# A graph layer with a Fourier-domain convolution: left-over products prepared beside the layer norm, a fourth bank and token halves in the last gate, set-up on ScalarE, weights read in 2 KB runs

## The chip, the cores and the metric

The kernel runs on one core of one Trainium2 chip. The time is the device time of one execution in microseconds; lower is better. All data are float32.

## The reference

The input is 32 images of 512 tokens with 256 features, and one 512 x 512 adjacency per image. Cut to what matters:

```
h = maximum(layernorm(x), 0)
c = relu(bn1(conv1(h)))                 # 1 tap, 256 -> 256 channels
c = bn2(conv2(c))                       # 17 taps along the tokens, 256 -> 256
x_conv = relu(c + h)
s = h @ w_se.T + b_se                   # 3 features
A = exp(-dist(s)) * adj
msg = relu(h @ w_msg.T + b_msg)
x_nmp = A @ msg
gi = concat(x_conv, x_nmp) @ w_ih.T + b_ih ; gh = h @ w_hh.T + b_hh
r = sigmoid(gi_r + gh_r) ; z = sigmoid(gi_z + gh_z)
n = tanh(gi_n + r * gh_n)
out = x + (1 - z) * n + z * h
```

## The kernel before, in words

The convolution with 17 taps is done in the frequency domain. The tokens are cut into windows of 64, transformed with length 80 by a matrix product, multiplied by transformed weights, and transformed back. 40 "units" of two spectrum rows each (a real and an imaginary part) stand for the 80 rows. The 32 images form two groups (g = 0, 1) of 16.

The stages follow each other as follows.

1. `first_part(0)`, about 0 to 176 us: for each image the layer norm (`statistics` and `normalise`: DVE, with a `pow` on POOL), the transpose of h on TensorE (`transpose_h`, tile `phT`), relu into `hT`, `conv1` and `windows_to_freq`. Between them `weights_to_freq` transforms the 17-tap weights (products `pw` from the taps `w2p`) and stores them into the DRAM buffer `WD` (in the profile `wd`), one row per spectrum row.
2. `nodes(0)`, to about 467 us: per image `message`, `features`, `factors`, `affinity`, `aggregate` for x_nmp, and between these the complex products of the units, `product(g, u)`. A product needs its unit's weights from `wd` (`load_unit`, an SP DMA into one of three `wt` buffers), their sum `wsum` and two tiles `both` (three POOL operations, `prepare`). Three units (`LEFT = 3`: 37, 38, 39) are left over.
3. `first_part(1)`, to about 604 us: the layer norm stage of the second group. The three left-over products are spread in it by the helper `fill`, to give TensorE work while the layer norm begins. Units 37 and 38 are prepared ahead of the stage; unit 39 is prepared, weights' load included, only where its product stands.
4. `nodes(1)`, to about 904 us, with all 40 products of the second group.
5. The "late" part, to the end: 16 pairs of images. `inverse` transforms back, `gates_rz` forms r and z, `gate_n` forms n. The three matrix products of a gate over a pair of images (2 x 2 blocks) are done with seven block products instead of eight (`Q1` to `Q7`); the helper `into` issues the three matmuls of one block product into a PSUM bank. A result (i, j) is feature half i of image j of the pair.

`blend` (L695) then takes d = h - n, multiplies it by z and adds n. `finish` turns the result to token order (`to_tokens`, a DVE transposition), adds it to x and stores it; `between(i)` calls it for the pair before. In the last pair, z comes last: `early_out` adds n to x beforehand, and the nested function `then` adds the z part. It uses `gates_rz` with `outs=[1]`, which holds three banks: b1 (Q1, Q2), b2 (Q6, Q7, Q4), b3 (Q5, Q3).

The order: parts 1, 3 and 5 are issued as written (`manual_schedule`); elsewhere a scheduler orders the instructions. Each engine takes its instructions in order, as does each DMA queue (SP's, ScalarE's and POOL's). A DMA that waits holds up what is behind it on its queue. [...]

At set-up, bn1 is folded into conv1: `batch_norm` forms scale and shift per channel, four small products with `diag` matrices spread them over all partitions (`row1`), and `w1` is multiplied by the scale.

Lines that the text below speaks of: L110 loads of x; L160 to L182 the set-up; L237 `pw`; L250 stores into `wd`; L265 to L277 layer norm; L288, L289 transposes of h and relu (`hT`), L290 its store; L301 conv1; L328 loads of `wt`; L332 `wsum`; L345 and L346 `both`; L364 the units' products; L566 all gate products; L598 and L607 the sums u2 and u3 of two block products (both named u); L585 the last sum of a gate result, L581 its sigmoid; L674 h - n; L697 and L698 `blend`; L704 the transposition to tokens; L709 and L693 additions into x; L714 stores of the output; L765 the combination of the gate weights; L911 the multiplication by z in the last pair.

Of the kernel before, what the change touches and what calls it, by code (L numbers as in the profile page):

```python
# [57 lines left out]
def gnn_layer(  # L58
# [64 lines left out]
    load_rows(w1, w1T, nc.scalar)  # L123
# [24 lines left out]
    def vectors():  # L148

        for h in range(2):  # L150
            rows = slice(64 * h, 64 * (h + 1))
            nc.vector.tensor_copy(vech[rows].rearrange("p (m e) -> p e m", e=DC),
                                  vec2[rows].rearrange("p e (m h) -> p e m h", h=2)[..., h])
        for name in VEC:
            at[name] = vech[:, cols[name]]
        nc.vector.tensor_add(brz, at["b_ih"][:, : 2 * DC], at["b_hh"][:, : 2 * DC])
        batch_norm("bn2", scale2, shift2)

    def batch_norm(k, scale, shift):
        nc.vector.tensor_scalar(scale, at[k + "_v"], BN_EPS, None, op0=ALU.add)  # L160
        nc.gpsimd.tensor_tensor(scale, scale, minus_half[:, :DC], op=ALU.pow)
        nc.vector.tensor_mul(scale, scale, at[k + "_g"])
        nc.vector.tensor_mul(shift, at[k + "_m"], scale)
        nc.vector.tensor_sub(shift, at[k + "_b"], shift)

    scale1, shift1 = (consts.tile([P, DC], FP, name=f"bn1_{k}") for k in ("scale", "shift"))
    batch_norm("bn1", scale1, shift1)


    row1 = bank("row1")  # L170
    with tc.tile_pool(name="setup", bufs=2) as setup:
        ones = setup.tile([P, P], FP, name="ones", bufs=1)
        nc.vector.memset(ones, 1.0)
        for i, v in enumerate((scale1, shift1)):
            for c in range(DC):
                diag = setup.tile([P, P], FP, tag="diag", name=f"diag_{i}_{c}")
                nc.vector.tensor_scalar(diag, ident, v[:, c : c + 1], None, op0=ALU.mult)
                nc.tensor.matmul(row1[:, i * D + c * P : i * D + (c + 1) * P], ones, diag, start=True, stop=True)
    shift1_row = early.tile([P, D], FP, name="shift1_row")
    nc.vector.tensor_copy(shift1_row, row1[:, D : 2 * D])  # L180
    for c in range(DC):
        nc.vector.tensor_mul(w1[:, c, :], w1[:, c, :], row1[:, :D])  # L182
# [25 lines left out]
    WD = dram.tile([WROWS, D, D], FP, name="wd")  # L208
# [18 lines left out]
    def weights_to_freq(gen, pc, i):  # L227
# [19 lines left out]
        if s + per == SI:  # L247
            for q in range(4):
                i0 = QI * q + PI * pc + i + per - SI
                nc.sync.dma_start(WD[:, i0 : i0 + SI, :], WST[q])  # L250
# [74 lines left out]
    def load_unit(g, u):  # L325
        t = WT[g, u] = wts.tile([P, 2, DC, D], FP, tag="wt", name=f"wt_{g}_{u}")
        for k in range(2):
            nc.sync.dma_start(t[:, k], WD[2 * u + k].rearrange("(i p) o -> p i o", p=P))  # L328
# [234 lines left out]
    def into(bk, q, o, ks, terms, first):  # L563

        for i, k in enumerate(ks):
            nc.tensor.matmul(bk, sw[:, k, q, o, :], terms[k][q], start=(first and i == 0), stop=(i == len(ks) - 1),  # L566
# [5 lines left out]
    def gates_rz(p, terms, between, outs=range(2), then=lambda i, j: None):  # L572
# [10 lines left out]
        def result(bk, other, o, i, j):  # L583
# [3 lines left out]
            then(i, j)  # L587
# [11 lines left out]
        for o in outs:  # L599
            into(b1[o], Q2, o, ks, terms, False)  # L600
            sigmoid(b1[o], o, 0, 0)
            then(0, 0)
# [13 lines left out]
        for o in outs:  # L616
            into(b3[o], Q3, o, ks, terms, False)
            result(b3[o], u2[o], o, 0, 1)

    def gate_n(p, terms, last):  # L620
# [51 lines left out]
        for i, j in ((0, 0), (1, 1), (1, 0), (0, 1)):  # L672
# [4 lines left out]
            elif not last:  # L677
                blend(p, i, j)
# [11 lines left out]
    def late_out(p, i, j, engine):  # L690
        half = slice(32 * i, 32 * (i + 1))
        x = XP[p][j][:, :, half]
        engine.tensor_tensor(x, x, OUT[p, j][:, :, half], op=ALU.add)  # L693

    def blend(p, i, j):  # L695
        n, d = NT[p][:, i, j, :], RZ[p][:, i, j, :]
        nc.vector.tensor_mul(d, d, RZ[p][:, DC + i, j, :])  # L697
        nc.vector.tensor_add(n, n, d)  # L698
# [13 lines left out]
    def store(p, j, queues):  # L712
        for g in range(4):
            queues[g % len(queues)].dma_start(quarter(out[2 * p + j], g), XP[p][j][32 * g : 32 * (g + 1)])  # L714
# [6 lines left out]
    def first_part(g, freq, between, left=()):  # L721
# [7 lines left out]
        normalise(b0)  # L729
        left = list(left)  # L730

        def fill():
            if left:
                left.pop(0)()
# [4 lines left out]
        normalise(b0 + 1)  # L739
        for b in range(b0, b1):  # L740
            if b + 3 < b1:
                load_x(b + 3, nc.gpsimd)
            if b == b0:
                conv1(b)
                if g == 0:
                    for steps in between(0):
                        for step in steps:
                            step()
                fill()
# [33 lines left out]
    with tc.tile_pool(name="freq", bufs=1) as fpool:  # L783
# [63 lines left out]
        with phase("pw"):  # L847
            with phase("nodes"):
                nodes(0, xf, range(UNITS - LEFT), GB)
            with phase("first", "sums"):  # L850
# [10 lines left out]
                left = [partial(product, pools["pw"], 0, u, xf) for u in range(UNITS - LEFT, UNITS)]  # L861
                for u in range(UNITS - LEFT, UNITS - LEFT + 2):
                    prepare(pools["pw"], 0, u, xf)
# [7 lines left out]
    with phase("late"), phase("sw"), phase("ops", bufs=2), phase("work"), tc.manual_schedule():  # L871
# [9 lines left out]
        for p in range(pairs):  # L881
# [19 lines left out]
            else:  # L901


                def then(i, j):

                    d = RZ[p]
                    if (i, j) == (0, 1):
                        to_tokens(p, 0, 1, d[:, 1, 0, :])
                        late_out(p, 1, 0, nc.gpsimd)
                        store(p, 0, [nc.sync, nc.scalar])  # L910
                    nc.vector.tensor_mul(d[:, i, j, :], d[:, i, j, :], d[:, DC + i, j, :])  # L911
                    if (i, j) != (1, 0):
                        to_tokens(p, j, i, d[:, i, j, :])
                        late_out(p, i, j, nc.vector)
                    if (i, j) == (0, 1):
                        store(p, 1, [nc.sync, nc.scalar])

                gates_rz(p, terms, between, [0])
                gate_n(p, terms, True)

                def between(i):
                    early_out(p, 1 - i, 1)

                gates_rz(p, terms, between, [1], then)
# [38 lines left out]
```

## Time and profile before

| | |
|---|---|
| median of 3 runs | 1900.99 us (1900.66 to 1903.49) |
| the profiled execution, its own time | 1902.63 us |
| its span, first to last instruction | 1900.8 us |
| TensorE busy | 1849.6 us (97%) |
| VectorE (DVE) busy | 1085.9 us (57%) |
| ScalarE (ACT) busy | 597.9 us (31%) |
| GpSimd (POOL) busy | 578.3 us (30%) |
| DMA | 309.9 MB, mean 163 GB/s |
| mean granted TensorE clock | 0.990 |

The profile names instructions by line, engine, operation and tiles, written as output<-input. PE is TensorE, PEld its weight loads. In lists of waits the columns are: the engine and line that waited, what it waited for, us in total, number of times, longest. In a timeline they are: start in us, duration in us, engine, line, operation, tiles, shapes, count of merged instructions, and in brackets the idle time before and what ended it. In a table by stage they are: the stretch, its length, then for PE, PEld, DVE, ACT and POOL the busy time with the number of instructions, then the granted TensorE clock as a share of full speed, the busy share of the DMA engines, and GB/s. A list of one line's instructions gives minimum, median and maximum duration in ns.

### The profile page before, as it was taken

The page shows a single profiled execution, that of the slowest core. Times are in us where ns is not written, and L with a number is a line of the kernel's source. Part 1 is how long each engine was busy: PE and PEld are TensorE (multiplying, and loading weights), DVE is VectorE, ACT ScalarE, POOL GpSimd, SP SyncE. Part 2 cuts the span into 40 slices and gives each one's busy share as a digit, 9 for nine tenths or more (in the row PEclk, how much of TensorE's full clock was granted, in tenths as well). Part 3 has the DMA queues.
Part 4 walks back from the last instruction along what each step waited for, and adds up shares of the span by engine and source line. Part 5 has one row for each costly group of instructions (what it writes and reads, how often), then busy time and mean ns, then how long its engine had stood idle before and what let it go on. Part 6 is the DMA issues. An engine that isn't in the chain of part 4 may idle for free.

```text
span 1900.8 us, 20925 instructions
## 1 busy us (share of the span) xinstructions
PE 1849.6 (97%) x6976; PEld 1113.0 (59%) x6976; DVE 1085.9 (57%) x2170; ACT 597.9 (31%) x1147; POOL 578.3 (30%) x558
## 2 busy tenths in 40 slices
PE   7999999999799999999999999999999999999997
PEld 5767566665698667665545554555455554555443
DVE  6874645544685544544265456655665456655666
ACT  2456444433235434443212221222212221222121
POOL 3331333434332334444422322133212322133210
PEclk9999999999899999999999999999999999999999
DMA  7999998776467998888532554235522554245512
GB/s 204 295 266 232 250 264 239 225 218 205 150 238 194 251 268 260 235 227 245 164 83 52 126 131 117 53 92 130 130 77 54 130 130 104 59 98 130 130 27 40
DMA packets 336953, 309.89 MB, mean 163 GB/s; under 512 B 148567, under 2 KB 286711, under 8 KB 336463
## 3 DMA queue, kind: packets, MB, share of 16 engines
q1 hardware_dynamic: 310175, 232.09, 48.0%
q10 hardware_dynamic: 18992, 49.17, 7.3%
q0 software_dynamic: 7680, 27.30, 5.3%
q8 instruction: 56, 0.92, 0.2%
q14 instruction: 50, 0.41, 0.1%
HBM read 201.60 MB, written 106.89 MB: 162 GB/s over the span
## 4 chain that ended last, share of the span: by engine, by line
PE 82%; DVE 3%; DMA 1%; issue 1%; POOL 1%; ACT 0%; SPq 0%; DVEq 0%; POOLq 0%; ACTq 0%
PE pg L566 30%; PE pn L566 15%; PE pn L457 11%; PE py L364 10%; PE pc L555 6%; PE pm L408 5%; PE pc L301 2%; PE pd L443 2%; PE px L316 1%; DMA ws<-w 1%; PE psr L432 1%; PE phT L288 0%; DVE xn L277 0%; DVE stats L265 0%; DMA yd<-y 0%
## 5 line engine op out<-in xcount | busy, mean ns | idle before, releaser
L544 POOL TENSOR_TENSOR hp<-hp 128x512 f32<-128x512 f32 x64 | 95.4, 1501 | 463.0 <-DMA hp<-hd 419.7
L566 PE MATMUL pg<-hp,sw 128*128 128x512 f32 x448 | 229.8, 595 | 3.1 <-DVE u L598 3.1
L566 PE MATMUL pg<-np,sw 128*128 128x512 f32 x448 | 229.6, 594 | 0.0
L566 PE MATMUL pg<-cp,sw 128*128 128x512 f32 x448 | 228.8, 592 | 0.0
L457 PE MATMUL pn<-A,msg 128*128 128x512 f32 x512 | 225.0, 592 | 0.0
L457 PEld LDWEIGHTS pn<-A,msg 128*128 128x128 f32 x512 | 97.1, 190 | 110.6 <-issue 107.9
L364 PE MATMUL py<-wt,both 128*128 128x256 f32 x624 | 152.3, 387 | 9.0 <-POOL both L346 8.3
L581 ACT ACTIVATE rz<-rz,brz 128x512 f32<-128x512 f32 x96 | 69.3, 722 | 277.0 <-DVE rz L585 277.0
L345 POOL TENSOR_TENSOR both<-xf 128x256 f32<-128x256 f32 x78 | 60.8, 780 | 314.0 <-PE py L364 281.2
L566 PEld LDWEIGHTS pg<-hp,sw 128*128 128x128 f32 x448 | 85.0, 190 | 110.3 <-issue 100.2
L566 PEld LDWEIGHTS pg<-np,sw 128*128 128x128 f32 x448 | 85.4, 191 | 107.7 <-issue 107.7
L566 PEld LDWEIGHTS pg<-cp,sw 128*128 128x128 f32 x448 | 85.3, 190 | 107.7 <-issue 107.7
L364 PEld LDWEIGHTS py<-wt,both 128*128 128x128 f32 x624 | 115.2, 192 | 52.3 <-issue 27.3
L544 POOL TENSOR_TENSOR cp<-cp 128x512 f32<-128x512 f32 x64 | 80.5, 1268 | 183.7 <-ACT cp L560 182.5
L449 DVE TENSOR_TENSOR A<-e,at 128x512 f32<-128x512 f32 x128 | 109.2, 892 | 42.0 <-ACT e L446 41.9
L332 POOL TENSOR_TENSOR wsum<-wt 128x512 f32<-128x512 f32 x78 | 107.8, 1383 | 70.5 <-DMA wt<-wd 64.7
L301 PE MATMUL pc<-w,hT 128*128 128x256 f32 x512 | 123.6, 397 | 3.1 <-DVE hT L289 3.1
L370 DVE COPY y<-py 128x256 f32<-128x256 f32 x78 | 32.8, 420 | 157.1 <-PE py L364 148.9
L555 PEld LDWEIGHTS pc<-back,yt 120*128 120x128 f32 x1024 | 116.9, 192 | 7.7 <-issue 7.7
L643 ACT ACTIVATE nt<-nt,vech 128x512 f32<-128x512 f32 x64 | 46.2, 722 | 234.3 <-DVE nt L642 234.3
L408 PE MATMUL pm<-wmsg,hq 128*128 128x259 f32 x512 | 117.3, 381 | 1.3 <-ACT hq L394 1.3
L555 PE MATMUL pc<-back,yt 120*128 120x80 f32 (+1 forms) x1024 | 116.2, 274 | 0.0
(123 smaller groups left out, 2935.5 us busy)
## 6 DMA issues: line engine op xcount, KB each, us to landing
wt<-wd SPq DMA_DIRECT2D x160, 256.0 KB, 4.7
adj<-in_adj_dram SPq DMA_DIRECT2D x128, 256.0 KB, 6.2
yd<-y ACTq DMA_DIRECT2D x80, 384.0 KB, 4.9
yt<-yd SPq DMA_DIRECT2D x60, 480.0 KB, 7.7
wd<-wst SPq DMA_DIRECT2D x64, 320.0 KB, 5.0
hd<-hT SPq DMA_DIRECT2D x32, 512.0 KB, 4.5
nd<-nmp ACTq DMA_DIRECT2D x32, 512.0 KB, 4.2
xb<-in_x_dram SPq DMA_DIRECT2D x128, 128.0 KB, 3.2
```

Of the source, the lines that this page charges most:

```text
L301: nc.tensor.matmul(p[:, j, :], HT[b][:, ic, c * P : (c + 1) * P], w1[:, ic, :], start=(ic == 0), stop=(ic == DC - 1))
L332: nc.gpsimd.tensor_tensor(t, WT[g, u][:, 0], WT[g, u][:, 1], op=ALU.add)
L345: nc.gpsimd.tensor_tensor(both[:, 0], re, im, op=ALU.add)
L364: nc.tensor.matmul(dst, v[:, ic, :], w[:, ic, :], start=(ic == 0), stop=(ic == DC - 1))
L408: nc.tensor.matmul(p[:, : D + NS], hq[:, ic, c * P : (c + 1) * P], wmsg[:, ic, :], start=(ic == 0), stop=(ic == DC - 1))
L449: nc.vector.tensor_mul(A[b][:, mc, :], e, at)
L457: nc.tensor.matmul(p, MSG[b][:, mc, dc * P : (dc + 1) * P], A[b][:, mc, :], start=(mc == 0), stop=(mc == NC - 1))
L544: nc.gpsimd.tensor_tensor(t[:, dst, :], t[:, a, :], t[:, b, :], op=sub)
L555: nc.tensor.matmul(bk[:, t0:t1], YT[p][j * W + w][:, oc * P : (oc + 1) * P], back[:, u0 : u0 + t1 - t0], start=(w == 0), stop=(w == W - 1) ...
L566: nc.tensor.matmul(bk, sw[:, k, q, o, :], terms[k][q], start=(first and i == 0), stop=(i == len(ks) - 1), skip_group_check=True)
L581: nc.scalar.activation(rz[:, g, j, :], src, AF.Sigmoid, bias=brz[:, g : g + 1], scale=1.0)
L643: nc.scalar.activation(n, n, AF.Tanh, bias=b_in[:, i : i + 1], scale=1.0)
```

## The change

There are five edits.

1. *Left-over products.* Unit 37 is prepared ahead of `first_part(1)`, and the weights of 38 and 39 are loaded there. 38 is prepared behind the first image's normalise, 39 behind the second's. `fill` now takes lists of steps and is called once more. The product of 39 stands where it stood, behind the second transposition.
2. *Last gate.* A function `last_z` replaces `gates_rz(p, terms, between, [1], then)`. It uses a fourth bank (Q4 goes into b4), takes Q4 ahead of Q5, and splits the last block product Q3 into two halves of the tokens; each half is blended, transposed, added and stored by itself. Nothing of this is on POOL any more.
3. *Blend.* In pair 14 (`B // 2 - 2`), two of the four blends, (1, 0) and (0, 1), go to POOL.
4. *Set-up.* bn1 is formed on POOL and the `diag` matrices on ScalarE; the copy of shift goes to ScalarE. In `first_part(0)` the scaling of w1 stands behind the first normalise, and the first taps' `weights_to_freq` ahead of the first conv1.
5. *Weights in 2 KB runs.* Partition p now holds channels 2p and 2p+1 of a unit, and not p and p+128, so that its two rows of 1 KB lie side by side in `wd`. conv1's output channels are put in the same order when w1 is scaled (`by_parity`). A row of `wd` is 4 KB longer than it needs.

```diff
     w1 = early.tile([P, DC, D], FP, name="w1")
-    load_rows(w1, w1T, nc.scalar)
+    w1_in = early.tile([P, DC, D], FP, name="w1_in")
+    load_rows(w1_in, w1T, nc.scalar)
...
-    batch_norm("bn1", scale1, shift1)
+    batch_norm("bn1", scale1, shift1, nc.gpsimd)
...
+    def bn1_row(i, v):
+        for c in range(DC):
+            diag = pools["setup"].tile([P, P], FP, tag="diag", name=f"diag_{i}_{c}")
+            nc.scalar.activation(diag, ident, AF.Copy, scale=v[:, c : c + 1])
+            nc.tensor.matmul(row1[i][:, c * P : (c + 1) * P], ones, diag, start=True, stop=True)
+
+    def scale_w1():
+        for c in range(DC):
+            nc.vector.tensor_mul(w1[:, c, :].rearrange("p (i q) -> p i q", i=DC), by_parity(w1_in[:, c, :]),
+                                 by_parity(row1[0][:, :D]))
...
-    WD = dram.tile([WROWS, D, D], FP, name="wd")
+    WD = dram.tile([WROWS, D * D + 4 * D], FP, name="wd")
...
-            nc.sync.dma_start(t[:, k], WD[2 * u + k].rearrange("(i p) o -> p i o", p=P))
+            nc.sync.dma_start(t[:, k], WD[2 * u + k, : D * D].rearrange("(p i o) -> p i o", i=DC, o=D))
...
+    def last_z(p, terms):
+
+        d, o, ks = RZ[p], 1, range(K3)
+
+        def blended(src, other, i, j, t=slice(0, N)):
+            z, dst = d[:, DC + i, j, t], d[:, i, j, t]
+            if other is not None:
+                nc.vector.tensor_add(z, other[:, t], src[:, t])
+                src = z
+            g = DC + i
+            nc.scalar.activation(z, src, AF.Sigmoid, bias=brz[:, g : g + 1], scale=1.0)
+            nc.vector.tensor_mul(dst, dst, z)
+            js, half = slice(t.start // 32, t.stop // 32), slice(32 * i, 32 * (i + 1))
...
+            nc.vector.transpose(OUT[p, j][:, js, half], dst.rearrange("p (j k) -> p j k", k=32))
+            x = XP[p][j][:, js, half]
+            nc.vector.tensor_add(x, x, OUT[p, j][:, js, half])
+
+        b1, b2, b3, b4 = (bank(f"pz{k}_{p}") for k in range(1, 5))
...
+        into(b4, Q4, o, ks, terms, True)
+        blended(b4, u3, 1, 0)
+        store(p, 0, [nc.sync, nc.scalar])
+        into(b3, Q5, o, ks, terms, True)
+        blended(b3, u3, 1, 1)
+        for h in range(2):
+            t = slice(h * N // 2, (h + 1) * N // 2)
+            into(b3, Q3, o, ks, terms, False, t)
+            blended(b3, u2, 0, 1, t)
+            store(p, 1, [nc.sync, nc.scalar], t)
...
-                blend(p, i, j)
+                blend(p, i, j, nc.gpsimd if p == B // 2 - 2 and i != j else nc.vector)
...
+        if g == 0:
+            scale_w1()
+            shift_w1()
...
         fill()
         statistics(b0 + 1)
         transpose_h(b0)
         normalise(b0 + 1)
+        fill()
         for b in range(b0, b1):
             if b + 3 < b1:
                 load_x(b + 3, nc.gpsimd)
             if b == b0:
-                conv1(b)
                 if g == 0:
                     for steps in between(0):
                         for step in steps:
                             step()
+                conv1(b)
                 fill()
...
-                left = [partial(product, pools["pw"], 0, u, xf) for u in range(UNITS - LEFT, UNITS)]
-                for u in range(UNITS - LEFT, UNITS - LEFT + 2):
-                    prepare(pools["pw"], 0, u, xf)
+                pw, (u0, u1, u2) = pools["pw"], range(UNITS - LEFT, UNITS)
+                left = [[partial(prepare, pw, 0, u1, xf), partial(product, pw, 0, u0, xf)],
+                        [partial(prepare, pw, 0, u2, xf)],
+                        [partial(product, pw, 0, u1, xf)],
+                        [partial(product, pw, 0, u2, xf)]]
+                prepare(pw, 0, u0, xf)
+                load_unit(0, u1)
+                load_unit(0, u2)
```

## The prediction

> **What bounds the kernel now.** I read the engine shares first, then TensorE's own waits, then the table by stage around each wait, then the timeline inside them.
>
> ```profile
> PE 1849.6 (97%) x6976; PEld 1113.0 (59%) x6976; DVE 1085.9 (57%) x2170; ACT 597.9 (31%) x1147; POOL 578.3 (30%) x558
> PEclk9999999999899999999999999999999999999999
> ...
> PE row L178 <- DVE diag L177: 9.2, 1, 9.2
> PE py L364 <- POOL both L346: 8.3, 1, 8.3
> PE phT L288 <- DVE xn L277: 8.0, 3, 3.5
> PE pc L301 <- DVE hT L289: 3.1, 2, 2.0
> PE pg L566 <- DVE u L598: 3.1, 1, 3.1
> ```
>
> TensorE is busy 1849.6 of 1900.8 us, so all that can be won without removing products is 51 us of idle time plus time lost at a low clock. About 11.3 of the 51 lie behind the last product (1889.5 to 1900.8) and 9.2 ahead of the first. The rest is a handful of single waits, and the edits sit on these: 8.3 us for a left-over product, 2.6 and 2.0 us around the layer norm, 3.1 us in the last pair's gate. The table by stage adds the clock (the number after the five busy times):
>
> ```profile
> 476.00:484.00 8.00, 7.07 (x20) 5.78 (x21) 3.93 (x9) 0.63 (x1) 1.77 (x2) 0.58 0.45 145
> 495.00:500.00 5.00, 4.75 (x12) 3.83 (x13) 2.45 (x11) 0.00 (x0) 1.14 (x3) 0.52 0.33 105
> 500.00:560.00 60.00, 60.00 (x373) 56.16 (x372) 54.01 (x146) 24.70 (x58) 23.89 (x26) 1.00 0.56 190
> 1841.00:1846.00 5.00, 4.89 (x8) 2.10 (x9) 2.81 (x5) 0.23 (x1) 0.00 (x0) 0.66 0.28 58
> ```
>
> After each of these waits TensorE works at half clock for some microseconds, so a wait costs more than its length. From 500 us on it is full again: what is won before that is carried to the end.
>
> **Part 1: the left-over products.** Now, in the timeline:
>
> ```profile
> 468.23 1.27 POOL L332 TENSOR_TENSOR wsum<-wt 128x512 f32<-128x512 f32 x1 [5.19 <-PE py L364]
> 471.61 1.04 POOL L271 TENSOR_TENSOR rstd<-rstd,minus_half 128x4 f32<-128x4 f32 x1
> 488.32 1.25 SPq L328 DMA_DIRECT2D wt<-wd  x2
> 492.57 1.26 POOL L332 TENSOR_TENSOR wsum<-wt 128x512 f32<-128x512 f32 x1 [4.73 <-DMA wt<-wd]
> 495.25 3.78 PE L364 MATMUL py<-wt,both 128*128 128x256 f32 x8 [8.31 <-POOL both L346]
> ```
>
> Unit 39's weights are issued on SP behind the second store of hT, which waits for the layer norm; then come landing, POOL's sum and two "both", and only then the product. After the change SP holds that load ahead of both hT stores. It waits only for a weight buffer (unit 36's product, 468.1). With the longest landing of that load in the trace (8.7 us) and POOL's 1.27+0.73+0.72 it is ready by 480; more likely POOL reaches it behind the second rstd, at 476.7 to 479.4. The product is due at 486.5, so the cover is at least 6 us. TensorE's path from the end of unit 38 and the transposes (486.94) to the next transposes (500.16) is 13.2 us; a warm product is 12 records in 2.79 us. Gain 13.2-2.8 = **10.4 us** (8.3 of waiting, 2.3 of low clock: the 12 records took 5.08).
>
> In front of it, POOL does the first rstd before unit 38's sums: rstd starts about 470.6 and not 471.61, **1.0 us** earlier. But unit 38's POOL work (2.7 us) now runs beside the four xn on DVE. The row for xn:
>
> ```profile
> L277 DVE TENSOR_SCALAR xn<-x,mv,rstd x128: 394/408/1095, 8.4 to 587.4; 128x256 f32<-128x256 f32 x128
> L709 DVE TENSOR_TENSOR xb<-xb,o x30: 1224/1226/2278, 985.8 to 1847.6; 128x1024 f32<-128x1024 f32 x30
> ```
>
> Beside POOL work (508.5, 573.2) four xn took 2.0 to 2.1 us, alone 1.4: I give back 0.6. Net 0.4. Behind: the load of x for image 19 moves past unit 39's sums on POOL, from 477.2 to about 479.4; with 0.8 of issue and a median landing of 7.1 it is there at 487.3, needed about 489. Cover 1.9 us; if the landing takes 10, 1 us comes back. Part 1: **10.8** (8 to 14; the upper end if the two shorter waits around the layer norm no longer drop the clock, worth 2.9, the 6.54 us of 16 conv records against 3.62).
>
> **Part 2: the second to last blend.** In pair 14 two of four blends (L697, L698) go to POOL.
>
> ```profile
> 1839.04 0.69 DVE L697 TENSOR_TENSOR rz<-rz 128x512 f32<-128x512 f32 x1
> 1839.76 0.69 DVE L698 TENSOR_TENSOR nt<-nt,rz 128x512 f32<-128x512 f32 x1
> 1840.37 0.68 DVE L598 TENSOR_TENSOR u<-p,pg 128x512 f32<-128x512 f32 x1
> 1841.11 2.00 PE L566 MATMUL pg<-hp,sw 128*128 128x512 f32 x2 [3.12 <-DVE u L598]
> ```
>
> TensorE waits because u (L598) must read a bank before the next product goes into it, and u stands behind twelve DVE instructions of the blends. Four of them leave, at steps of about 0.7: u ends at 1838.3, the wait falls from 3.12 to 0.4, gain 2.7. After the wait two matmuls (hp, np) step by 1.75 us where 0.86 is normal: 1.8 more.
> The Trainium skill ("SBUF — State Buffer", Who interferes with whom) speaks against this edit: VectorE with two SBUF inputs and GpSimd reading SBUF exclude each other for the whole instruction, and whoever comes first wins. The row agrees in kind: L709 takes 1.23 alone and up to 2.28. By the rule, if POOL's first multiply (1.27) gets in ahead of the last subtraction (L674), u is 1.3 late and the gain 1.4 smaller. I think the subtraction, which follows back to back, wins; u itself reads PSUM and is 0.68 beside POOL too. Then finish(14, .) transposes wait for POOL's blends (ready about 1840.2 and 1842.7 to 1844 where DVE would be at 1839.0 and 1842), and the first z/r result reads its bank late: TensorE meets it at Q3, up to 1 us. Sum 2.7+1.8-0.8 = **3.7** (2 to 4.7).
> The same skill ("TensorE: Matmul & The Clock Gate", What you observe and What's actually happening) says the clock halves after an idle window of about 3.4 us, on windows that run freely. Trace: 0.50 after 3.12 us. By the rule a 0.4 us gap keeps the clock (4.5 before deductions); if it did not, 2.7. I take the rule's sum.
>
> **Part 3: set-up.** DVE loses four diag (0.28), four small bn1 operations (0.15) and a copy (0.41). POOL gains four small operations. None is in the trace there; the nearest are the pow of the same shape, 0.73, and a memset of 0.10; I take 0.4, so shift is ready about 10.4 and not 9.2. The diag on ScalarE are taken as 0.3 (its 128x256 copy is 0.38), behind the table load (5.8 to 7.1), which is done by then. The first transposes stand behind the row of shift, near 11.5 as now (11.46). The eight tap products move ahead of the first conv (14.25): their weights' last DMA is issued on SP at 9.8 and lands after 4 to 8 us, 13.5 to 17.7. The later copies of wst, which today delay the third image's statistics (22.94), are then done earlier; I expect about 21.7 for these. At 13.5 the gain is 1.3, at 17.7 the loss 3. I take **+0.7** (-3 to +2). The strided multiplies into w1 are once 0.37 each; double would be hidden in the wait for hT.
>
> **Part 4: the tail.** 18 matmuls of 512 columns and 6 of 256 replace 21 of 512: a 256-column record steps by 0.22, a 512 one by 0.43, so TensorE ends the same. DVE until 1885.03 is unchanged. From there it is the bound:
>
> ```profile
> 1892.04 1.25 POOL L693 TENSOR_TENSOR xb<-xb,o 128x512 f32<-128x512 f32 x1 [74.33 <-DVE o L704]
> 1892.13 1.71 DVE L911 TENSOR_TENSOR rz<-rz 128x512 f32<-128x512 f32 x1 [0.17 <-ACT rz L581]
> 1893.32 3.42 SPq L714 DMA_DIRECT2D out_dram<-xb  x4
> 1893.88 0.71 DVE L704 STREAM_TRANSPOSE o<-rz 128x512 f32<-128x512 f32 x1
> 1894.62 0.69 DVE L693 TENSOR_TENSOR xb<-xb,o 128x512 f32<-128x512 f32 x1
> ```
>
> The POOL add that held a multiply for 1.0 us goes, but its add (0.69) comes to DVE, and each blended() runs add, sigmoid, multiply, transpose, add in order with nothing in between. Two full chains (3.55 each) bring DVE to 1892.1; a half chain is 0.41 x4 and a sigmoid near 0.46, with gaps 2.25; two are 4.5, and ACT's store issues between the sigmoids (2 x 0.42) cost about 0.4. Last add ends about 1897.0, against 1895.31: 1.7 worse. But image 30 is stored from 1888.7 and no longer beside image 31, and the last store is half. Now 5.5 us pass from the last add to the end, for 1 MB in all; the landings of the stores are 2.5 to 4.0, and with 0.8 of issue I take 3.5. Net **+0.3** (-1.5 to +1.5).
>
> **Part 5: 2 KB runs.** 41 MB in 160 loads; their waits (POOL wsum, 64.7 us in 27 waits) reach TensorE almost nowhere: it idles 3 us in all between 604 and 890. Hidden behind other products: **+0.3** (-0.5 to +1.5, from 3 us of small waits at 176 to 205, where the DMA share is 0.9 and more).
>
> **Sum.** 10.8+3.7+0.7+0.3+0.3 = 15.8. Span 1900.8 lies in an execution of 1902.63, so 1886.8 for it; the median of the runs is 1900.99, 1.64 lower: **1885.2**.
>
> **The rivals.**
> - *Given back* (17%): POOL and DVE exclude each other as the rule has it (-1.4), the tap weights land late (-3 and not +0.7), x of image 19 arrives late (-1). Then 9.7 us remain: about 1891.3, range 1889.5 to 1895. For it: the L709 row. Against: three small things at once.
> - *Clock kept at the layer norm* (8%): 2.9 more and a good set-up: about 1881. Against: the waits there still add to over 3 us within 6.
> - *Slower* (5%): the weights' new place. Rows of wd now lie 260 KB apart, and each partition takes one 2 KB run. If such a load landed slower, the three weight buffers set the pace: a buffer comes round in about 20 us (three products a batch, 19.95 us a batch), less 2.7 of POOL and 2.8 of TensorE, so it decides from a landing of about 14 us, three times the 4.7 of now. Each us beyond it is paid in some 25 rounds: 15.5 us of landing gives -38+16, about 1923. Against: longer runs should not triple a landing.
> - *It does not do what it says*: the third product would still wait if SP's load stood behind hT; in the instruction order it does not. I give it nothing of its own.
>
> **Numbers.** Main case 70%, 1881 to 1889.5. Range 1880.0 to 1890.5: it leaves out the worst of the first rival, the slower one and a little on the low side. About 0.2% (3.8 us) is what a measurement of this kernel can tell from no change. Faster 0.92, same 0.03, slower 0.05.
>
> **What would show it.** TensorE's waits lose the 8.3 line; the product of unit 39 follows the transposes at about 486 at full clock; the granted clock in the last pair's first gate stays 1.00; DVE's last add comes 7 to 8 us after the last matmul, not 5.8. I am wrong if TensorE waits for phT or stats in the layer norm after 490, if conv1 starts after 17 at the start, or if landings of wt grow.

## The result, and the profile after

| | before | after |
|---|---|---|
| median | 1900.83 us (6 runs, 1900.25 to 1905.64) | 1889.66 us (6 runs, 1884.57 to 1894.78) |
| profiled execution, its own time | 1902.63 us | 1885.27 us |
| its span | 1900.8 us | 1883.5 us |
| mean granted clock of TensorE | 0.990 | 0.994 |

The ratio of the times is 0.9935, with a 95% interval from 0.9913 to 0.9958: faster. The forecast was 1885.2 us with a range of 1880.0 to 1890.5. A second set of five runs of the same kernel gave 1887.36; all eleven together have a median of 1887.82, from 1884.57 to 1894.78. So the gain is 11.2 us between the medians of the table (1900.83 - 1889.66) and 13.2 us with all eleven runs (1900.99 - 1887.82). The 13.2 us are used below, as they rest on more runs. The 17.4 us between the two profiled executions are too much, because the profiled execution of the changed kernel is one of the quickest.

The shares of the engines and the granted clock in 40 slices, from the page of the changed kernel:

```profile
PE 1844.1 (98%) x6982; PEld 1110.4 (59%) x6982; DVE 1084.0 (58%) x2162; ACT 599.9 (32%) x1153; POOL 583.1 (31%) x565
PEclk9999999999999999999999999999999999999999
```

TensorE's busy time fell by 5.5 us although six records were added, since fewer records ran at a low clock (the mean granted clock is 0.994 where it was 0.990). Its longest waits (engine and line that waited, what for, us in all, times, longest):

```profile
PE row L187 <- ACT diag L186: 10.2, 1, 10.2
PE phT L305 <- DVE xn L294: 8.8, 5, 3.4
PE pz L583 <- DVE rz L642: 3.2, 2, 2.4
PE psl L444 <- DVE fr L439: 2.0, 2, 1.0
PE pc L318 <- DVE hT L306: 1.5, 1, 1.5
```

Of the two lines that the change aimed at, the 8.3 us for `both` are gone and the 3.1 us for u are down to 0.2. A new one is there: 3.2 us for rz in the last gate. The table by stage, for the layer norm of the second group (two stretches), a stretch behind the blends of the second to last pair, and the end:

```profile
466.00:476.00 10.00, 5.61 (x15) 4.00 (x16) 9.01 (x19) 0.09 (x1) 7.32 (x9) 0.61 0.56 220
476.00:484.00 8.00, 8.00 (x37) 6.86 (x36) 5.53 (x17) 1.90 (x4) 2.16 (x4) 0.85 0.24 93
1830.00:1835.00 5.00, 4.48 (x11) 1.82 (x10) 2.91 (x4) 1.33 (x2) 0.00 (x0) 1.00 0.75 158
1872.00:1883.50 11.50, 3.69 (x11) 2.19 (x10) 5.35 (x11) 1.30 (x3) 0.00 (x0) 0.80 0.40 82
```

In the layer norm TensorE is still busy for only 5.6 of 10 us, at clock 0.61; in the second stretch it is busy all the time. The timeline of that place:

```profile
465.88 1.03 POOL L288 TENSOR_TENSOR rstd<-rstd,minus_half 128x4 f32<-128x4 f32 x1 [7.10 <-DVE rstd L287]
466.90 1.25 POOL L349 TENSOR_TENSOR wsum<-wt 128x512 f32<-128x512 f32 x1
466.95 3.14 DVE L294 TENSOR_SCALAR xn<-x,mv,rstd 128x256 f32<-128x256 f32 x4 [1.15 <-POOL rstd L288]
472.96 6.36 PE L318 MATMUL pc<-w,hT 128*128 128x256 f32 x16 [1.48 <-DVE hT L306]
481.75 1.04 PE L305 MATMUL phT<-ident,xn 128*128 128x128 f32 x8
482.62 1.89 PE L381 MATMUL py<-wt,both 128*128 128x256 f32 x8
485.21 1.04 PE L305 MATMUL phT<-ident,xn 128*128 128x128 f32 x8
```

Unit 39's product (482.62) follows the transposes with no bracket, so with no wait, and the next transposes come 3.5 us after the last ones (481.75) where it was 14.3. But four xn take 3.14 us beside the three POOL operations of `prepare` (`wsum` and two `both`), against 1.4 alone. From the first product behind the last aggregation to the transposes behind unit 39's product it was 34.83 us (465.33 to 500.16) and is 25.15 (460.06 to 485.21): 9.7 us in place.

At the blends of the second to last pair:

```profile
1821.96 1.28 DVE L733 TENSOR_TENSOR rz<-hp,nt 128x512 f32<-128x512 f32 x2
1822.72 1.65 POOL L752 TENSOR_TENSOR rz<-rz 128x512 f32<-128x512 f32 x1 [19.31 <-DVE rz L733]
1823.16 0.68 DVE L614 TENSOR_TENSOR u<-p,pg 128x512 f32<-128x512 f32 x1
1823.89 1.13 PE L583 MATMUL pg<-hp,sw 128*128 128x512 f32 x2 [0.22 <-DVE u L614]
1827.03 2.13 POOL L753 TENSOR_TENSOR nt<-nt,rz 128x512 f32<-128x512 f32 x1
1832.41 1.12 PE L583 MATMUL pg<-hp,sw 128*128 128x512 f32 x2 [0.52 <-DVE rz L602]
```

VectorE's subtractions (L733) come first and run undisturbed, POOL's first multiply is stretched to 1.65 us, u comes in time, and the wait is 0.22 us instead of 3.12. The clock behind it is 1.00 (1824 to 1829), where it was 0.66 before. A later bank is read late (0.52 us).

The end:

```profile
1860.84 1.07 PE L583 MATMUL pz<-hp,sw 128*128 128x512 f32 x2
1866.91 0.68 DVE L642 TENSOR_TENSOR rz<-u_z,pz 128x512 f32<-128x512 f32 x1
1869.85 0.69 DVE L652 TENSOR_TENSOR xb<-xb,o 128x512 f32<-128x512 f32 x1
1870.46 0.68 DVE L642 TENSOR_TENSOR rz<-u_z,pz 128x512 f32<-128x512 f32 x1
1871.19 1.22 PE L583 MATMUL pz<-hp,sw 128*128 128x256 f32 x2 [2.42 <-DVE rz L642]
1874.86 0.70 PE L583 MATMUL pz<-hp,sw 128*128 128x256 f32 x2 [0.74 <-DVE rz L642]
1877.70 0.51 ACT L645 ACTIVATE rz<-rz,brz 128x256 f32<-128x256 f32 x1 [2.35 <-DVE rz L642]
1879.18 0.42 DVE L652 TENSOR_TENSOR xb<-xb,o 128x256 f32<-128x256 f32 x1
```

TensorE waits twice, 2.42 and 0.74 us, for the sum L642, and the first of these sums (1870.46) runs only behind the last add of the block before (1869.85). The last sigmoid (1877.70) starts 0.6 us after its sum has ended; ScalarE was issuing two stores until then. Counted from the start of z's second block product (Q2, 1860.84), ahead of which both tails are alike, the end of the program came 21.84 us later before (1878.96 to 1900.8) and comes 22.66 us later now (1860.84 to 1883.5). The new tail loses 0.8 us. Other profiles agree: 21.99 to 22.2 us in three more with the old tail, 22.6 to 23.3 in four more with the new one.

### The profile page after: what moved, and what is told of

Same layout as the page of the kernel before. It is cut to its first block, busy times and chain, and to the rows that moved or that the text cites. A ratio compares the mean times of both kernels' runs of the same rounds, so it can differ in the third digit from the quotient of the medians.

```text
span 1883.5 us, 20947 instructions
## 1 busy us (share of the span) xinstructions
PE 1844.1 (98%) x6982; PEld 1110.4 (59%) x6982; DVE 1084.0 (58%) x2162; ACT 599.9 (32%) x1153; POOL 583.1 (31%) x565
## 2 busy tenths in 40 slices
DMA packets 316537, 309.89 MB, mean 165 GB/s; under 512 B 148631, under 2 KB 245815, under 8 KB 316047
## 4 chain that ended last, share of the span: by engine, by line
PE 91%; issue 2%; DVE 2%; DMA 2%; POOL 1%; ACT 1%; SPq 0%; POOLq 0%; ACTq 0%; DVEq 0%
PE pg L583 29%; PE pn L583 14%; PE pn L474 11%; PE py L381 11%; PE pc L572 6%; PE pm L425 6%; PE pc L318 5%; PE px L333 3%; PE pw L254 2%; PE pd L460 2%; PE phT L305 1%; PE psr L449 1%; DMA hT<-hd 1%; DVE stats L282 0%; PE pz L583 0%
## 5 line engine op out<-in xcount | busy, mean ns | idle before, releaser
L583 PE MATMUL pg<-hp,sw 128*128 128x512 f32 x434 | 221.9, 593 | 0.7 <-DVE rz L602 0.5
L583 PE MATMUL pg<-cp,sw 128*128 128x512 f32 x434 | 221.6, 592 | 0.0
L583 PE MATMUL pg<-np,sw 128*128 128x512 f32 x434 | 221.6, 592 | 0.0
```

The costliest lines, as they stand in the source:

```text
L583: nc.tensor.matmul(bk[:, t], sw[:, k, q, o, :], terms[k][q][:, t], start=(first and i == 0), stop=(i == len(ks) - 1), skip_group_check=True)
```

## The experiments

The kernel before was run again beside these, with medians of 1900.99 to 1902.35 us.

**The changed kernel once more**, with no edit, to learn how much two profiles of one kernel differ.

> The changed kernel once more, for a second trace and more times. Its six times so far lie from 1884.6 to 1894.8 us, and the first trace is of one of 1885.3. Theory A (clock): the spread is time at half clock behind the short waits (16 conv1 records in 3.6 or 6.4 us, the last pair's first gate). Then two traces differ in the granted clock of the stretches at 20 to 30, 465 to 484 and 1822 to 1835, by up to 5 us, and nowhere else by over 1 us. Theory B (DMA): the spread is landings in the node stages; then the two traces differ in TensorE's waits between 60 and 460 or 590 and 890 us. Median expected between 1885 and 1892.

Measured: 1887.36 us (1885.83 to 1888.46), ratio 0.9924 (0.9909 to 0.9940), clock 0.996 in the profile. The waits in the last gate are the same to the hundredth (2.42 and 0.74), and four xn take 3.14 us again. Two things differ. The 16 products of the second group's convolution take 5.14 us at a granted clock of 0.71, where they took 6.36 at 0.56. And the wait in front of the transposes is 4.44 us and not 3.04, because the load of x landed later. The first line is of the changed kernel's profile, the second of this one:

```profile
463.91 1.40 DVE L282 BATCH_NORM_STATS2 stats<-x 128x6 f32<-128x256 f32 x4 [2.30 <-DMA x<-in_x_dram]
467.13 1.41 DVE L282 BATCH_NORM_STATS2 stats<-x 128x6 f32<-128x256 f32 x4 [3.70 <-DMA x<-in_x_dram]
```

So the waits that come from the order of instructions are repeated; those for a load, and the clock, are not.

**Part 1 alone**, on the kernel before:

```diff
+                pw, (u0, u1, u2) = pools["pw"], range(UNITS - LEFT, UNITS)
+                left = [[partial(prepare, pw, 0, u1, xf), partial(product, pw, 0, u0, xf)],
+                        [partial(prepare, pw, 0, u2, xf)],
+                        [partial(product, pw, 0, u1, xf)],
+                        [partial(product, pw, 0, u2, xf)]]
+                prepare(pw, 0, u0, xf)
+                load_unit(0, u1)
+                load_unit(0, u2)
```

> The kernel before with the left-over products' edit alone (part 1 of the sum). Theory A (the prediction's part 1, corrected by the xn that took 3.1 us beside POOL and not 2.0): the 8.3 us wait for both is gone, transposes of the third image of the group come 9.5 to 10 us earlier, time 1891 median, 9 to 10.5 below before. Rival (given back): a load of x or a stall at the combination of the gate weights takes 3 us or more of it, time 1894 or more.

Measured: 1890.24 us (1890.07 to 1893.82) against 1901.05 of before: 10.8 us, ratio 0.9944 (0.9926 to 0.9962). In place, its profile is 1.6 us behind the profile of before at the entry of the layer norm (472.3 against 470.68) and 9.0 us ahead for the transposes near the stage's end (565.46 against 574.43): 10.6 us. One edit gives most of the result, at the size that the sum gave it. Its set-up is that of before, instruction for instruction, and yet:

```profile
14.02 3.89 PE L301 MATMUL pc<-w,hT 128*128 128x256 f32 x16 [1.09 <-DVE hT L289]
24.45 2.30 PE L288 MATMUL phT<-ident,xn 128*128 128x128 f32 x8 [3.53 <-DVE xn L277]
```

In the profile of before the same 16 products took 5.80 us, and the third image's transposes came at 26.59. The same code differs by 2.1 us there. That the products ran at another pace is plain, but not why. The table by stage has a clock of 1.00 there for both profiles (the first line is of before, the second of this run), although 5.80 us are a good half more than the 3.62 that 16 such products take at full clock elsewhere:

```profile
15.00:17.00 2.00, 2.00 (x7) 1.55 (x6) 1.31 (x4) 0.00 (x0) 2.00 (x4) 1.00 0.69 248
15.00:17.00 2.00, 2.00 (x11) 1.77 (x10) 1.77 (x4) 0.06 (x1) 2.00 (x5) 1.00 0.83 262
```

**Preparing later**: in the changed kernel, unit 38's POOL work goes behind unit 37's product and so behind the first four xn.

```diff
-                left = [[partial(prepare, pw, 0, u1, xf), partial(product, pw, 0, u0, xf)],
-                        [partial(prepare, pw, 0, u2, xf)],
-                        [partial(product, pw, 0, u1, xf)],
+                left = [[partial(product, pw, 0, u0, xf)],
+                        [partial(prepare, pw, 0, u1, xf)],
+                        [partial(prepare, pw, 0, u2, xf), partial(product, pw, 0, u1, xf)],
```

> The changed kernel with unit 38 prepared on POOL only behind the second image's normalise, and unit 39 behind the first conv1. Theory A (POOL holds the shared access, so that the first image's four xn took 3.14 us and not 1.38): xn is back at 1.4 us, the first transposes start about 1 us earlier and end 1.7 us earlier, and the time is 1.7 to 2 us lower than the changed kernel's; up to 5 lower if conv1 then keeps its clock. Rival (the chain is paced by something else, the load of x or the statistics): xn short but transposes no earlier, no change; or unit 39 comes late and TensorE waits 1 us or more for it.

Measured: 1886.79 us (1881.48 to 1890.19), 1.0 us below the eleven runs. The timeline has the first image's xn back at their old length, and a wait of 1.92 us in front of the transposes:

```profile
469.80 1.38 DVE L294 TENSOR_SCALAR xn<-x,mv,rstd 128x256 f32<-128x256 f32 x4 [1.16 <-POOL rstd L288]
470.36 1.64 PE L305 MATMUL phT<-ident,xn 128*128 128x128 f32 x8 [1.92 <-DVE xn L294]
```

So the 1.76 us by which xn grew do come from POOL's sums beside it. The load of x differs from profile to profile, so I count from the statistics of the first image to conv1. That takes 9.05 us (9.04 once) in all six profiles of kernels that prepare early, 7.29 and 7.28 in the two with this order (the second is a kernel below), 8.27 in the profile of before, and 7.29 in that of the 2 KB runs alone (below), which has the order of before but in which x came later, when POOL was free. The front of part 1 therefore lost 0.8 us, or 1.8 against the latter profile, where I had counted on a gain of 0.4. Preparing later wins the 1.76 us back but not for good: the second image's xn now take 4.88 us and not 3.14, and from conv1 to the next product it is 6.6 and 6.4 us, where it was 5.0 to 6.3 in the six. The median moves by less than runs of one kernel do.

**The last gate in turns**: the chains of blended() are cut up so that each sum that frees a bank goes ahead of the multiply, transpose and add of the block before (`first` is sum and sigmoid, `times` the multiply, `turned` transpose and add).

```diff
-        blended(b4, u3, 1, 0)
-        store(p, 0, [nc.sync, nc.scalar])
+        first(b4, u3, 1, 0)
         into(b3, Q5, o, ks, terms, True)
-        blended(b3, u3, 1, 1)
-        for h in range(2):
...
+        times(1, 0)
+        first(b3, u3, 1, 1)
+        turned(1, 0)
+        store(p, 0, [nc.sync])
+        into(b3, Q3, o, ks, terms, False, ha)
...
```

> The changed kernel with the operations of its last gate put in turns: the sum of (1, 1) ahead of the transposition of (1, 0), each half's sum ahead of the transposition of the part before, the first half's store on SP alone. The same instructions, in another order. Theory A (the tail is bound by DVE's order, TensorE waits 2.4 and 0.7 us for sums that release bank b3 while DVE waits 0.6 to 1.2 us for each sigmoid): TensorE's waits fall to under 1 us in all, the last add comes about 3 us earlier, time 2.5 to 3.5 us below the changed kernel. Rival (DVE is full anyway, or the store's landing sets the end): under 1 us.

Measured: 1886.91 us (1883.64 to 1889.88), 0.9 us below the eleven runs where 2.5 to 3.5 were expected.

```profile
1870.39 0.68 DVE L642 TENSOR_TENSOR rz<-u_z,pz 128x512 f32<-128x512 f32 x1
1872.47 0.68 DVE L642 TENSOR_TENSOR rz<-u_z,pz 128x512 f32<-128x512 f32 x1
1873.20 0.70 PE L583 MATMUL pz<-hp,sw 128*128 128x256 f32 x2 [0.94 <-DVE rz L642]
1875.48 0.70 PE L583 MATMUL pz<-hp,sw 128*128 128x256 f32 x2 [0.72 <-DVE rz L642]
```

The second sum follows the first after 2.08 us and not 3.55 (1866.91 to 1870.46 in the changed kernel), and TensorE's first wait falls from 2.42 to 0.94. The records behind it are at full clock: 0.70 us for two, where the changed kernel shows 1.22. The last add ends 15.3 us after the start of Q2, 3.5 us earlier than in the changed kernel, as expected. The end comes 20.7 us after the start of Q2 (1864.32 to 1885.0): 2.0 us earlier than with the new tail, 1.2 earlier than with the old. So 1.5 us are lost again behind the last add, where the stores land (5.4 us from it to the end, against 3.9). TensorE's waits add to 1.66 us, not to under 1. The late release of the bank is most of what held the new tail, but not all: this run also takes the first half's store off ScalarE, and the last sigmoid starts 0.5 us after the start of its sum and not 1.0.

**2 KB runs alone**, on the kernel before:

```diff
-            nc.sync.dma_start(t[:, k], WD[2 * u + k].rearrange("(i p) o -> p i o", p=P))
+            nc.sync.dma_start(t[:, k], WD[2 * u + k, : D * D].rearrange("(p i o) -> p i o", i=DC, o=D))
```

(with the stores, the padding of `wd` and the order of w1's channels that go with it)

> The kernel before with part 5 alone: unit weights read in 2 KB runs, rows of wd 4 KB longer, w1 scaled into parity order. Theory A (the prediction's part 5, +0.3): TensorE's waits in the first group's nodes stage hardly move; time 1900 to 1901. Rival (longer runs relieve the DMA engines where they are busiest, 176 to 216 us, and with them the loads of hT and adj): small waits at 176 to 216 fall from 3 us to under 1.5, time 1.5 to 2 us below before; POOL's wait for wt falls from 64.7 to about 45 us either way.

Measured: 1902.2 us in 10 runs, ratio 1.0006 (0.9992 to 1.0019): nothing. Its page shows that the runs did become longer, 316,473 DMA packets and not 336,953 for the same 309.89 MB. The median landing of a load of wt is 4.4 us (before 4.7). POOL's wait for wt fell from 64.7 to 49.0 us, TensorE's waits between 176 and 216 us from 3.1 to 2.3, where the rival had them under 1.5.

**All blends on VectorE again**, in the changed kernel:

```diff
-                blend(p, i, j, nc.gpsimd if p == B // 2 - 2 and i != j else nc.vector)
+                blend(p, i, j, nc.vector)
```

> The changed kernel with all four blends of pair 14 on DVE again (part 2 undone). Theory A (part 2): TensorE's wait of 3.1 us for u is back at about 1824, a spell at half clock may follow it; from there the rest is 3.1 to 4.9 us later, less the 0.5 us wait that the POOL blends bring. Time 2.5 to 4.5 us above the changed kernel. Rival: the wait comes back but the tail, which DVE sets, swallows it: under 1 us.

Measured: 1892.26 us (1890.42 to 1897.88), 4.4 us above the eleven runs of the changed kernel, with ranges that overlap. In place it is plain: from the first matmul of n's gate in pair 14 to the same matmul in pair 15 it is 41.19 us here and before, and 37.37 or 37.38 in three profiles with two blends on POOL. The wait is back, and the records behind it are slow again (two np matmuls took 1.02 us in the changed kernel's timeline):

```profile
1831.00 1.12 PE L583 MATMUL pg<-hp,sw 128*128 128x512 f32 x2 [3.12 <-DVE u L614]
1831.96 1.46 PE L583 MATMUL pg<-np,sw 128*128 128x512 f32 x2
1833.22 1.91 PE L583 MATMUL pg<-cp,sw 128*128 128x512 f32 x2
```

**Both better**: preparing later and the last gate in turns together, on the changed kernel.

> The changed kernel with the last gate's operations in turns and units 38 and 39 prepared later, both at once. In the traces of each alone, the layer norm stage was 2.5 us shorter and the tail 1.9 us shorter than in the changed kernel at the same clock. Theory A: they add, 4.4 us below the changed kernel, median 1883 to 1885 with a spread of up to 8 us from spells at half clock. Rival: one takes the other's gain, 2 us or less.

Measured: 1885.11 us (1880.61 to 1888.51), ratio 0.9912 (0.9897 to 0.9926). That is 2.7 us below the eleven runs, where 4.4 were expected if the two gains add. The tail is 20.6 us from the start of Q2, 2.1 less than in the changed kernel. From the statistics to the transposes behind unit 39's product it is 19.8 us, against 20.1 to 21.4 in the six that prepare early. The ranges of the runs overlap.

**Kept warm**: the last one, with useless products put into three of TensorE's waits.

```diff
+    def keep_warm(name, n):
+        p = bank(name)
+        for _ in range(n):
+            nc.tensor.matmul(p, ident, w1.rearrange("p c d -> p (c d)"), start=True, stop=True)
```

> The kernel of both edits (e7) with matmuls of no use put into three waits: 3 of 128x512 ahead of the third image's transposes at about 21 us, 2 ahead of the first transposes of the second group, 2 ahead of its first conv1 (0.86 us each at full clock, into a bank that nobody reads). They add work to TensorE and take none away. Theory A (the spread between executions, and some 5 us of the median, are spells at half clock that follow short waits): the granted clock at 20 to 40 and 465 to 484 is 0.95 or more, 16 conv1 records behind the waits take about 3.7 us and not 6.4, time 3 to 6 us below e7 and a spread of under 4 us. Rival (the windows of the clock run freely, and the other waits drop it as often): the spread stays, and the time is the same or up to 2 us higher, by the matmuls added.

Measured: 1882.18 us (1881.72 to 1886.24), ratio 0.9903 (0.9889 to 0.9916), the lowest median of all versions. It is 2.9 us below the kernel without the useless products, where 3 to 6 were expected; the four runs spread over 4.5 us.

```profile
465.34 1.88 PE L796 MATMUL warm<-w,ident 128*128 128x512 f32 x4
467.11 1.64 PE L305 MATMUL phT<-ident,xn 128*128 128x128 f32 x8
468.59 1.88 PE L796 MATMUL warm<-w,ident 128*128 128x512 f32 x4
470.70 3.89 PE L318 MATMUL pc<-w,hT 128*128 128x256 f32 x16 [0.23 <-DVE hT L306]
```

The table by stage has for it:

```profile
466.00:476.00 10.00, 9.77 (x39) 6.24 (x38) 9.42 (x21) 0.18 (x1) 6.35 (x8) 1.00 0.50 192
```

The clock is 1.00 where it was 0.61, and the convolution takes 3.89 us for 16 products. From the first product behind the last aggregation to the end of that convolution it is 14.3 us (460.16 to 474.43), in the kernel without the useless products 18.4 (465.68 to 484.07). Of these 4.1 us 2.8 are left at the second image's convolution, because the transposes ahead of it now wait for xn.

**The old tail**: the changed kernel with the last gate put back to three banks and the old order.

```diff
-                last_z(p, terms)
+                gates_rz(p, terms, between, [1], then)
```

> The changed kernel with only the last gate put back to three banks and to the old order of its token halves (everything else changed). Theory: the new tail is not a gain but a small loss, since the third product of the first half writes into a bank that still holds the fifth product of the other half until VectorE, behind the whole chain of the first half, has read it. Then TensorE's waits for rz in the last gate (2.42 and 0.74 us in the changed kernel's profile) are gone or under 0.5 us together, and the time from the start of z's second product to the end of the program is about 21.8 us as in the kernel before, against 22.7; the median is some 0.8 us lower than the changed kernel's, 1886 to 1888. Rival, the tail as predicted (a gain of 1 to 2 us hidden by something else in that profile): the stretch becomes longer than 22.7 us. A difference of 0.8 us is less than the medians can tell, so the stretch decides.

Measured: 1886.34 us (1883.98 to 1893.18). TensorE's waits for rz in the last gate are gone, and from the start of Q2 to the end it is 21.99 us (1860.21 to 1882.2) against 22.66. In place the old tail is 0.7 us better; the medians cannot show it.

**The changed kernel kept warm**: its own order, with the useless products only.

> The changed kernel with useless products (weights by the identity, into a bank that nobody reads) put into three of TensorE's waits: 3 at about 21 us, 3 before the transposes of the second group's layer norm, 2 before its convolution. Nothing else is changed, and the outputs are the same. Theory: the spells of low granted clock that follow these waits are what the changed kernel's median has over its profiled execution, and most of its spread: with TensorE kept busy there is no stretch below 0.97 from 15 to 50 us and from 460 to 490 us, the second group's convolution takes 3.9 us for 16 products instead of 6.4, the mean clock is 0.996 or more, the median 1883 to 1885, 3 to 5 us below the changed kernel's. Rival, the fillers only take time (the clock is given or withheld for other reasons, or the fillers themselves delay what follows): no difference or up to 2 us slower, with the spells still there.

Measured: 1885.28 us (1881.88 to 1894.44), 2.5 us below the eleven runs of the changed kernel where 3 to 5 were expected, and the spread did not shrink. The profiled execution was the slowest of the seven, which makes it instructive:

```profile
90.00:110.00 20.00, 17.53 (x81) 12.43 (x78) 11.93 (x32) 8.74 (x19) 6.13 (x9) 0.74 0.81 235
230.00:240.00 10.00, 8.46 (x27) 4.98 (x26) 5.95 (x17) 5.64 (x12) 2.21 (x2) 0.83 0.99 225
478.00:490.00 12.00, 11.19 (x43) 6.92 (x42) 10.99 (x23) 1.51 (x4) 8.13 (x9) 1.00 0.48 180
```

Where the useless products stand (478 to 490) the clock is full, and the stretch to the end of the convolution is 15.7 us (472.89 to 488.59) against 19.1 (460.06 to 479.16; 17.1 to 19.3 in five profiles with that order). But the execution was 12.8 us behind when it came there. The clock dropped at 90 to 110, behind a wait of 2.47 us for h, and at 230, where nothing was added. And some 4.5 us were lost ahead of the first useless product:

```profile
14.80 3.72 PE L254 MATMUL pw<-w2p,taps 17*80 17x512 f32 x16
18.45 6.11 PE L318 MATMUL pc<-w,hT 128*128 128x256 f32 x16
```

In the changed kernel's profile these took 2.03 and 3.72 us. The clock rows have 1.00 here too, so they do not show the cause. The fillers work in their place; a run that loses time elsewhere is as slow as before.

## Why the prediction was right, point by point

- *Part 1, 10.8.* Shown: 10.6 us in place when done alone, 10.8 between the medians. The step worth 10.4 us brought 10.8: between the two transposes around unit 39's product lay 14.26 us (485.90 to 500.16) and lie 3.46 (481.75 to 485.21). The step in front of it failed: I took 2.0 to 2.1 us for four xn beside POOL, from two rows in which POOL was busy for only part of the time. It is 3.14, so that the 1.0 us of the earlier rstd is more than used up: the front loses 0.8 us instead of gaining 0.4. The load of x for image 19 came in time (its statistics at 485.42 follow with no wait), though the cover was 1.7 us by the prediction's own figures (489 - 487.3) and not 1.9. The Trainium skill ("SBUF — State Buffer", Who interferes with whom) counts tensor_scalar among the operations that can take the pair of ports shared with GpSimd, each engine then blocking the other for a whole instruction. I had used the rule for the blends and not for xn. By it xn alternates with POOL's operations. Preparing later shows that POOL's work is the cause, and the rows agree with the rule, though no run shows the ports themselves: four xn take 1.38 us alone, 3.14 beside three POOL operations, and 4.87 where five stand beside them in the kept-warm kernel.
- *Part 2, 3.7.* 3.8 us in place (41.19 to 37.37: the wait from 3.12 to 0.22, no slow records behind it, a late bank for 0.52), the same 3.8 in place by undoing it, and 4.4 between the medians. The bet that the subtraction gets to the port first held: POOL paid, with 1.65 and 2.13 us for operations of 1.27.
- *Part 3, +0.7 (-3 to +2).* Not settled. The products behind a wait for h near 90 us begin at 91.92 to 93.02 in three profiles with the old set-up, and at 89.45 to 94.36 in seven with the new one (means 92.6 and 90.9). The same code differs by 2.1 us at 14 to 24 us, so an effect of this size cannot be read from these profiles. One step did fail: the first transposes behind the row of shift were to stay near 11.5, and begin at 12.80 (11.46 before), since the first row product starts at 10.2 to 10.9 in nine profiles with the new set-up and at 8.9 to 9.5 in three with the old one. And a sign of being wrong that I had named, conv1 after 17 us, did show, in four of the nine (17.13 to 18.45). What stays of 13.2 us when the other parts are taken out (10.6 + 3.8 - 0.8 + 0) is -0.4.
- *Part 4, +0.3 (-1.5 to +1.5).* Measured -0.8. The step that failed is "TensorE ends the same". The new order takes Q4 ahead of Q5, and Q3 is added into b3, which still holds Q5 until VectorE has read it. That read stands behind the whole chain of the block before, so TensorE ends its last product 15.6 us after the start of Q2, and not 10.5 as before. Putting the old tail back took both waits away, and putting the reads first cut them to 0.94 and 0.72 us, so this is shown and not only argued. The rest of the step was close: the last add came 2.4 us later (I had 1.7), and the program ended 3.9 us behind it (I had 3.5, before 5.5). The sign that I gave for it, a last add 7 to 8 us behind the last matmul, fell with it: it was 3.2.
- *Part 5, +0.3.* Nothing (1.0006), as its cover said. The rival built on it, landings beyond 14 us, did not happen: 4.4 us in the median, 8.5 at most.
- *The sum and the median.* The point was 2.6 us too low against the eleven runs. The tail is 1.1 of it (from +0.3 to -0.8); the rest is within what the clock does from one execution to the next, over 10 us in the changed kernel, and is not assigned. The range held because it already had room for losses of that size, and on the six runs of the result with 0.8 us to spare. Their median, 1889.66, lies just outside the main case (1881 to 1889.5) and in the range of the rival *Given back* (1889.5 to 1895), but its three causes are not what the profile shows: POOL gave way to the subtraction, x of image 19 was in time, and the tap products follow the transposes with no wait (14.33). So the mechanism was right in parts 1 and 2, which bring the gain. That the small terms left the sum within the range was in part luck.

## What to carry to other kernels

A product that waits for its operands is best cured by starting their load and their preparation earlier, but count what the earlier work then stands beside: four elementwise operations on VectorE that last 1.4 us alone took 3.1 beside GpSimd. Where a chain of VectorE operations is written out block by block, put the read that frees a PSUM bank first; a fourth bank helps nothing while the last product still goes into one that is waiting to be read. And where runs of one kernel spread by more than the effect, read the effect from a stretch of the timeline with fixed ends, and from undoing the edit alone.

## What the runs showed of the hardware that was not expected

- The time of the same instructions differs between executions: eleven runs of one kernel lie between 1884.57 and 1894.78. In the layer norm the granted clock goes with it (16 products in 6.36 us at 0.56, in 5.14 at 0.71). At the start it does not: the first convolution took 5.80 or 3.89 us with 1.00 in the clock rows of both profiles. So full clock in a row does not prove that the products ran at full pace; their durations have to be read too.
- The Trainium skill ("TensorE: Matmul & The Clock Gate", What's actually happening) speaks of an idle window of about 3.4 us. Here the clock also fell behind single waits of 2.40 and 2.47 us near 90 us (0.74 over the 20 us from 90 on, in two profiles). If only a fully idle window of that length counted, neither would have cost more than its length, yet 16 products behind the first took 4.54 us where 3.62 is normal. The length of the wait does not decide alone either: at the same place the clock stayed at 1.00 with waits of 1.15 and 1.37 us, and fell to 0.91 over the 20 us with 0.96 and 1.33 us. What decides stays open.
- Useless products can pay: putting some into three waits took 2.9 us from one median and 2.5 from another. The stretch that holds two of the waits is 14.3 us with them against 17.5 and 18.4 in the two profiles of that order without, and 15.7 against 17.1 to 19.3 in five of the other order. The ranges of the runs overlap, so the medians alone do not prove it; the stretches do, for these places.
